# An expert layer behind linear attention: the last rows, the counting and the results in a new order of issue

## The chip, the cores and the metric

The kernel runs on one core of one Trainium2 chip. The time is the device time of the launch in microseconds (us). A change of about 0.2% (2.2 us) is the smallest that repeated runs of this kernel can tell from none.

## What is computed

Four sequences of 2,048 tokens with 256 channels go through a layer norm, a causal linear attention with 16 heads and a residual sum, and then through a second layer norm and a mixture of 8 experts, of which each token uses two.

```python
x = x + linear_attention(layernorm(x), Wq, bq, Wk, bk, Wv, bv, Wo, bo)   # elu(q)+1, elu(k)+1, causal
h = layernorm(x)
logits = h @ router_w.T                       # 8 experts
top, idx = top_k(logits, 2); p = softmax(top)
out = x + sum over the two chosen e of p_e * (gelu(h @ w1[e].T + b1[e]) @ w2[e].T + b2[e])
```

All of it is float32. The layer norms have no learned scale.

## The kernel before

**Blocks.** The 8,192 tokens are cut into 16 blocks of 512. A block goes through `stage_a` (layer norm, q, k, v, denominators), `stage_b` (scores, causal product, state) and `stage_c` (output projection `px` at L594, residual sum, choice of the two experts, second layer norm, counting). One pass `s` of the main loop (L968) traces stage a of block s, stage b of block s-1 and stage c of block s-2, piece by piece in turn; there are 18 passes, and the last one, s = 17, holds only stage c of block 15.

**Rows.** `stage_c` ends in a counting: two small products `pc` (L651, L654) of the choice `sel` with a triangular matrix and with ones give each token's place in its expert's list; VectorE turns them into `slots` (L675), and eight indirect DMAs on GpSimd's queue (L679) write the normed rows with token number and weights into `rows` in DRAM. These DMAs are collected in `writes`.

**Slot tiles.** The experts work on tiles of 256 rows of one expert. 68 of them are in the main program, three more stand behind a runtime condition at the end. A slot tile j is: `fetch_rows` (L797-L804: expert and row number into registers of SyncE, then the load of `xs`), `fetch_in` (L814, w1 of the expert, 512 KB), `fetch_out` (L822 and L826, w2 and b2), `turned` (four transposes `pt_xs` at L835 and the copy `xT` at L836), `hidden` (16 products `ph` at L863 and the gelu at L869), `output` (16 products `py` at L880, the sum with b2 at L885, the scaling at L889) and `store` (two indirect DMAs with addition, L894, that add the results into the output in DRAM). Every `store` waits until the two DMAs of the store before it have landed, and until the blocks' x1 that have been traced so far have landed (`after(i, added[-1] + stored)`). Every `fetch_rows` waits for all `writes` that have been traced before it. SyncE's queue runs in the order of tracing; the other engines' orders are made at build time by a scheduler that takes priorities from the order of tracing, and `follow` adds an order between two instructions without a wait.

**Order of tracing.** `slot_tiles` is a generator. For each j it does, up to the first yield, `hidden(j)`, `turned(j + 1)`, `fetch_rows(j + 3)`, `fetch_in(j + 2)`, and up to the second yield `output(j - 1)`, the store of tile j - 2, and `fetch_out(j + 1)`. `Work.step` runs it to the next yield. The main loop spreads the steps over the pieces of the passes: as many as the rows that are complete allow, `limit = 2 * (open_tiles - 3)`. Before pass 17 there are 49 open tiles and 84 steps have been run, so that the limit of 92 leaves 8; from these pass 17 takes off `2 * HOLD`, and the rest runs after the main loop, behind the tracing of the last block's rows:

```python
if s == NBLK + 1:
    left = max(0, left - 2 * HOLD)
```

**Buffers.** `xs`, `w1`, `w2` and `b2` have three buffers each, the result `y` four.

Of the kernel before, what the change touches and what calls it, by code (L numbers as in the profile page):

```python
# [13 lines left out]
ALU = mybir.AluOpType  # L14
# [10 lines left out]
def kernel(  # L25
# [132 lines left out]
    def ins_of(i):  # L158
        return getattr(i, "ins", i)

    def follow(inst, other):

        tc.add_manual_dep(
            ins_of(inst), ins_of(other).name,
            mybir.DependencyInfo(
                mybir.DependencyClass.NoSync, mybir.DependencyReason.SCHED_ONLY
            ), reason="order of issue",
        )

    QUIET = ROUND_ENDS[0] + 2  # L170

    def layernorm(src, dst, root_of=None, power=False, behind=None):

        st = small.tile([P, NT, 6], F32, tag="st", name="st")
        mv = small.tile([P, NT, 2], F32, tag="mv", name="mv")
        for t in range(NT):
            i = nc.vector.bn_stats(st[:, t, :], src[:, t, :])  # L179
            if behind:  # L180
                follow(i, behind[0])
            nc.vector.bn_aggr(mv[:, t, :], st[:, t, :])
        rstd = small.tile([P, NT], F32, tag="rstd", name="rstd")
        nc.vector.tensor_scalar_add(rstd, mv[:, :, 1], LN_EPS)
        if power:
            root = small.tile([P, NT], F32, tag="root", name="root")
            nc.gpsimd.tensor_tensor(root, rstd, neghalf, ALU.pow)
        else:

            half = small.tile([P, NT], I32, tag="half", name="half")  # L190
            nc.vector.tensor_single_scalar(
                half, rstd.bitcast(I32), 1, op=ALU.logical_shift_right
            )
            guess = small.tile([P, NT], I32, tag="guess", name="guess")
            nc.vector.tensor_scalar(guess, half, -1.0, float(0x5F3759DF), ALU.mult, ALU.add)
            root = guess.bitcast(F32)
            error = small.tile([P, NT], F32, tag="error", name="error")
            for _ in range(3):
                nc.vector.scalar_tensor_tensor(error, root, -0.5, root, ALU.mult, ALU.mult)
                nc.vector.tensor_tensor(error, error, rstd, ALU.mult)  # L200
                nc.vector.scalar_tensor_tensor(root, error, 1.5, root, ALU.add, ALU.mult)
        if root_of is not None:
            nc.vector.tensor_tensor(root_of, rstd, root, ALU.mult)
        rstd = root
        shift = small.tile([P, NT], F32, tag="shift", name="shift")
        i = nc.vector.scalar_tensor_tensor(
            shift, mv[:, :, 0], -1.0, rstd, ALU.mult, ALU.mult
        )
        if behind is not None:
            behind[:] = [i]  # L210
        for t in range(NT):
            if t % 2:
                nc.scalar.activation(  # L213
                    dst[:, t, :], src[:, t, :], AF.Identity,
                    bias=shift[:, t : t + 1], scale=rstd[:, t : t + 1],
                )
# [365 lines left out]
    def stage_c(n: int):  # L582
# [30 lines left out]
        for r in range(2):  # L613
            top = small.tile([P, NT], F32, tag=f"top{r}", name="top")
            nc.vector.tensor_reduce(top, lg, AX.X, ALU.max)
            eq = small.tile([P, NT, E], F32, tag=f"eq{r}", name="eq")
            nc.vector.tensor_tensor(eq, lg, wide(top), ALU.is_equal)
            nc.vector.tensor_tensor(eq, eq, prio_b, ALU.mult)
            first = small.tile([P, NT], F32, tag=f"first{r}", name="first")
            nc.vector.tensor_reduce(first, eq, AX.X, ALU.max)  # L620
            nc.vector.tensor_tensor(sel[:, :, r, :], eq, wide(first), ALU.is_equal)
            if r == 0:
                nc.vector.scalar_tensor_tensor(
                    lg, sel[:, :, 0, :], -3.0e38, lg, ALU.mult, ALU.add
                )
            tops.append(top)
        yield
        xn2 = att.tile([P, NT, R], F32, tag="xn2", bufs=3, name=f"xn2_{n}")
        rstd = layernorm(x1, xn2[:, :, 0:D])


        ed = small.tile([P, NT], F32, tag="ed", name="ed")
# [15 lines left out]
        sel_f = sel.rearrange("p t k e -> p (t k e)")  # L648
        M = 2 * NT
        pc = bank([P, 2, M, E], "pc")  # L650
        nc.tensor.matmul(  # L651
            pc[:, 0].rearrange("p m e -> p (m e)"), before, sel_f, start=True, stop=True
        )
        nc.tensor.matmul(  # L654
            pc[:, 1].rearrange("p m e -> p (m e)"), ones, sel_f, start=True, stop=True
        )
# [126 lines left out]


    plans = {}

    def slot_tiles(todo):

# [66 lines left out]
        def hidden(j):  # L855
            xT, w1t, bias = (state[j][key] for key in ("xs", "w1", "bias"))
            hT = moe.tile([P, NFC, ST], F32, tag="hT", name="hT")
            for f2 in range(NFC // 2):
                ph = bank([P, 2, ST], "ph")
                for i in range(2):  # L860
                    f = 2 * f2 + i
                    for cc in range(NCC):
                        nc.tensor.matmul(  # L863
                            ph[:, i, :], w1t[:, cc, ts(f, P)], xT[:, cc, :],
                            start=(cc == 0), stop=(cc == NCC - 1),
                        )
                for i in range(2):
                    f = 2 * f2 + i
                    nc.scalar.activation(  # L869
                        hT[:, f, :], ph[:, i, :], AF.Gelu, bias=bias[:, f : f + 1]  # L870
                    )
            state[j]["hT"] = hT

        def output(j):
            mine = state.pop(j)
            w2t, b2t, hT, to, wt = (mine[key] for key in ("w2", "b2", "hT", "to", "wt"))
            py = bank([P, NS, D], "py")
            for a in range(NS):
                for f in range(NFC):
                    nc.tensor.matmul(  # L880
                        py[:, a, :], hT[:, f, ts(a, P)], w2t[:, f, :],
                        start=(f == 0), stop=(f == NFC - 1),
                    )
            yt = moe.tile([P, NS, D], F32, tag="y", bufs=4, name=f"y_{j}")
            nc.vector.tensor_tensor(  # L885
                yt, py, b2t.unsqueeze(1).to_broadcast([P, NS, D]), ALU.add
            )
            for a in range(NS):
                nc.vector.tensor_scalar_mul(yt[:, a, :], yt[:, a, :], wt[:, a : a + 1])  # L889

            def store():
                mine = []
                for a in range(NS):
                    i = ins_of(nc.gpsimd.indirect_dma_start(  # L894
                        out=out_rows, in_=yt[:, a, :], in_offset=None, compute_op=ALU.add,
                        bounds_check=T - 1, oob_is_err=False,
                        out_offset=bass.IndirectOffsetOnAxis(ap=to[:, a : a + 1], axis=0),
                    ))

                    apart(i, f"out{len(added)}")  # L900
                    tc.add_to_no_dep_group("out", i)
                    after(i, added[-1] + stored)
                    mine.append(i)
                added.append(mine)

            return store
# [13 lines left out]
        for j in range(J + 1):  # L920
            if j < J:
                hidden(j)
            if j + 1 < J:
                turned(j + 1)
            if j + LEAD < J:
                fetch_rows(j + LEAD)
            if j + LEAD - 1 < J:
                fetch_in(j + LEAD - 1)
            if j < J:
                yield  # L930
            if j > 0:
                wait.append(output(j - 1))
            while len(wait) > (j < J):
                wait.pop(0)()
            if j + 1 < J:
                fetch_out(j + 1)
            if j < J:
                yield

    begins = {n - 1: r for r, n in enumerate(ROUND_ENDS)}
    HOLD = 5

    class Work:

# [21 lines left out]
    for s in range(NBLK + 2):  # L968
# [18 lines left out]
        while gens:  # L987
            for it in list(gens):
                if next(it, "end") == "end":
                    gens.remove(it)  # L990
                i += 1
                while ran < share and ran * order < i * share:
                    work.step()
                    ran += 1
# [58 lines left out]
```

## Time and profile before

| what | value |
|---|---|
| median of 4 runs | 1097.31 us (1096.05 to 1098.62) |
| the profiled execution's own time | 1101.44 us |
| its span, first to last instruction | 1099.7 us |
| TensorE busy, mean granted clock | 1022.6 us (93%), 0.957 |
| VectorE busy | 766.5 us (70%) |
| GpSimd busy (its indirect DMAs' issue) | 394.0 us (36%) |
| ScalarE busy | 385.3 us (35%) |
| store DMAs (L894) | 136, 1593 ns of GpSimd each, 4.4 us to landing |
| row DMAs (L679) | 128, 973 ns of GpSimd each, 2.6 us to landing |

The profile is one execution, and times inside it are counted from the start of its span. A line of the timeline has start, duration, engine, source line, operation, what is written from what, a count, and in brackets the idle time of the engine before it with what ended that idle time. A line of the table of waits has the waiting engine and line, what it waited for, the sum in us, how often, and the longest. In the table of windows each engine has its busy time and, in brackets, its instructions; behind them come the granted TensorE clock, the mean busy share of the 16 DMA engines and GB/s.

### The profile page before, as it was taken

The numbers are of one execution on the slowest core, as the hardware profiler recorded it, in microseconds if no ns is written. First come the engines' busy times: TensorE is split into PE (matmuls) and PEld (weight loads), VectorE is DVE, ScalarE is ACT, GpSimd is POOL, SyncE is SP. The second block draws the span as 40 slices with busy tenths as digits, with TensorE's granted clock in tenths as the row PEclk, the third lists the DMA queues.
The fourth block names the chain that finished last, engine by engine and source line by source line (L and its number), as shares of the span: only waits on it lengthen the run. The fifth ranks groups of instructions, "written<-read, shape, count | busy, mean of one in ns | idle before, by whom it ended". The sixth has DMA issues, their size and how long they took to land.

```text
span 1099.7 us, 23082 instructions
## 1 busy us (share of the span) xinstructions
PE 1022.6 (93%) x8358; PEld 816.0 (74%) x8358; DVE 766.5 (70%) x2600; ACT 385.3 (35%) x824; POOL 394.0 (36%) x308
## 2 busy tenths in 40 slices
PE   5897987989999999999999999999999889999993
PEld 3565665666767787878878887878788768888883
DVE  6769779879597959796888789796777633333331
ACT  3434333335252535243433435252532111222220
POOL 5003043132232444435351525243334543344434
PEclk9878988889899999999999999999999989999997
DMA  6001111534333556564646474645556589898873
GB/s 212 1 16 44 59 59 40 169 121 107 117 87 128 138 166 157 154 166 111 170 118 201 108 203 113 194 99 179 126 155 160 136 246 232 228 240 236 231 181 39
DMA packets 128722, 155.22 MB, mean 141 GB/s; under 512 B 9952, under 2 KB 105952, under 8 KB 128608
## 3 DMA queue, kind: packets, MB, share of 16 engines
q1 hardware_dynamic: 85680, 102.06, 29.7%
q0 software_dynamic: 25728, 34.88, 17.5%
q10 hardware_dynamic: 17200, 16.79, 4.8%
q8 instruction: 67, 1.10, 0.4%
q14 instruction: 47, 0.39, 0.1%
HBM read 108.05 MB, written 45.65 MB: 140 GB/s over the span
## 4 chain that ended last, share of the span: by engine, by line
PE 65%; DVE 22%; DMA 4%; issue 2%; POOL 1%; ACT 1%; SPq 0%; POOLq 0%; DVEq 0%
PE ph L863 19%; PE py L880 17%; DVE at L511 5%; PE pn L534 5%; PE pp L401 4%; PE sc L506 4%; DMA out_dram<-y,to 4%; PE pv L426 3%; PE px L594 3%; PE pn L527 3%; PE pt_xs L835 2%; DVE st L179 2%; DVE z L411 2%; PE pr L471 1%; DVE kT L343 1%
## 5 line engine op out<-in xcount | busy, mean ns | idle before, releaser
L894 POOL DMA_INDIRECT out_dram<-y,to x136 | 216.7, 1593 | 440.8 <-DVE y L885 121.0
L863 PE MATMUL ph<-xT,w 128*128 128x256 f32 x1088 | 256.2, 390 | 5.6 <-DMA w<-in_w_dram 5.2
L880 PE MATMUL py<-w,hT 128*128 128x256 f32 x1088 | 248.0, 381 | 0.0
L863 PEld LDWEIGHTS ph<-xT,w 128*128 128x128 f32 x1088 | 208.1, 195 | 41.9 <-issue 7.7
L880 PEld LDWEIGHTS py<-w,hT 128*128 128x128 f32 x1088 | 202.9, 190 | 28.7 <-issue 2.6
L869 ACT ACTIVATE hT<-ph,b1t 128x256 f32<-128x256 f32 x272 | 113.5, 469 | 223.2 <-PE ph L863 216.5
L511 DVE TENSOR_TENSOR at<-sc,causal 128x512 f32<-128x512 f32 x256 | 158.3, 679 | 11.1 <-PE sc L506 11.1
L679 POOL DMA_INDIRECT rows<-xn,slots x128 | 124.6, 973 | 94.0 <-DVE slots L675 51.4
L836 DVE COPY xT<-pt_xs 128x512 f32<-128x512 f32 x68 | 46.7, 687 | 143.3 <-PE pt_xs L835 143.3
L885 DVE TENSOR_TENSOR y<-py,b 128x512 f32<-128x512 f32 x68 | 47.0, 691 | 86.3 <-PE py L880 86.2
L506 PE MATMUL sc<-qM,kT 32*128 32x256 f32 x1024 | 79.2, 410 | 5.2 <-ACT share L436 5.2
L534 PE MATMUL pn<-at,vpad 128*32 128x128 f32 x2048 | 77.3, 297 | 0.0
L497 ACT ACTIVATE qM<-qs,parity 128x256 f32<-128x256 f32 x128 | 56.3, 498 | 58.3 <-DVE qs L476 46.1
L506 PEld LDWEIGHTS sc<-qM,kT 32*128 32x128 f32 x1024 | 49.4, 189 | 30.7 <-issue 8.2
L541 ACT COPY vT<-pn 128x256 f32<-128x256 f32 x64 | 23.7, 370 | 130.3 <-PE pn L534 130.3
L534 PEld LDWEIGHTS pn<-at,vpad 128*32 128x32 f32 x2048 | 57.6, 118 | 9.4 <-issue 2.0
L594 PE MATMUL px<-wo_sb,vT 128*128 128x264 f32 x256 | 64.1, 406 | 0.0
L426 PE MATMUL pv<-wv_sb,xnT 128*128 128x264 f32 x256 | 64.0, 406 | 0.0
L401 PE MATMUL pp<-xnT,wk_sb 128*128 128x512 f32 x128 | 60.3, 615 | 0.2 <-ACT xnT L336 0.2
L594 PEld LDWEIGHTS px<-wo_sb,vT 128*128 128x128 f32 x256 | 49.4, 198 | 12.7 <-issue 3.5
L232 POOL TENSOR_TENSOR x<-x,bo_bc 128x1024 f32<-128x1024 f32 x16 | 42.2, 2638 | 45.3 <-ACT xn L213 38.2
L401 PE MATMUL pp<-xnT,wq_sb 128*128 128x512 f32 x128 | 58.2, 597 | 0.0
(169 smaller groups left out, 1319.0 us busy)
## 6 DMA issues: line engine op xcount, KB each, us to landing
w<-in_w_dram SPq DMA_DIRECT2D x136, 512.0 KB, 4.6
xs<-rows SPq DMA_DIRECT2D x68, 260.0 KB, 3.0
b<-in_b_dram SPq DMA_DIRECT2D x68, 128.0 KB, 4.8
out_dram<-x ACTq DMA_DIRECT2D x16, 512.0 KB, 3.0
x<-in_x_dram ACTq DMA_DIRECT2D x15, 512.0 KB, 4.0
rows<-none SPq DMA_DIRECT2D x1, 2340.0 KB, 7.7
out_dram<-y,to POOLq DMA_INDIRECT x136, 4.4
rows<-xn,slots POOLq DMA_INDIRECT x128, 2.6
```

The source lines that it names most:

```text
L401: nc.tensor.matmul(pp, w[:, cc, ts(m, P)], xnT[:, cc, :], start=(cc == 0), stop=(cc == NCC - 1),)
L426: nc.tensor.matmul(pv, xnT[:, cc, ts(t, P)], wv_sb[:, cc, :], start=(cc == 0), stop=(cc == NCC - 1),)
L497: nc.scalar.activation(qM[:, :, par, :], qs[:, :, ts(c, P)], AF.Copy, scale=parity[:, par : par + 1],)
L506: nc.tensor.matmul(sc[g][:, m, :, :], kT[part, m, ts(c, P)], qM[part, m, :, :], start=True, stop=True,)
L511: nc.vector.tensor_tensor(at[:, g].rearrange("p m r i -> p (m r) i"), sc[g].rearrange("p m r i -> p (m r) i"), causal.unsqueeze(1).to_broa ...
L534: nc.tensor.matmul(pn[W * g : W * g + W, m, :], vp[:, c, NG * m + g, W * par : W * par + W], at[:, g, m, par, :], start=False, stop=(par = ...
L594: nc.tensor.matmul(px, vT[:, cc, ts(t, P)], wo_sb[:, cc, :], start=(cc == 0), stop=(cc == NCC - 1),)
L679: s = ins_of(nc.gpsimd.indirect_dma_start(out=rows[:, :], out_offset=bass.IndirectOffsetOnAxis(ap=slots[:, 2 * t + k : 2 * t + k + 1], axi ...
L863: nc.tensor.matmul(ph[:, i, :], w1t[:, cc, ts(f, P)], xT[:, cc, :], start=(cc == 0), stop=(cc == NCC - 1),)
L869: nc.scalar.activation(hT[:, f, :], ph[:, i, :], AF.Gelu, bias=bias[:, f : f + 1])
L880: nc.tensor.matmul(py[:, a, :], hT[:, f, ts(a, P)], w2t[:, f, :], start=(f == 0), stop=(f == NFC - 1),)
L894: i = ins_of(nc.gpsimd.indirect_dma_start(out=out_rows, in_=yt[:, a, :], in_offset=None, compute_op=ALU.add, bounds_check=T - 1, oob_is_er ...
```

## The change

Four edits. In the slot tiles, `fetch_rows(j + 3)` moves from the first half of step j to the end of the second, behind `fetch_in(j + 2)`, the store and `fetch_out(j + 1)`. In pass 17, `HOLD` is 7 in place of 5, and one step is run by hand after the second piece of stage c, which is the choice `sel`. For the last block, the second layer norm's reciprocal root is put behind the choice on VectorE, and the first counting product behind the last slot tile product that has been traced. Every store that is traced after the last block's rows is put behind the last of their DMAs on GpSimd's queue.

```diff
-    def layernorm(src, dst, root_of=None, power=False, behind=None):
+    def layernorm(src, dst, root_of=None, power=False, behind=None, last=None):
...
-        nc.vector.tensor_scalar_add(rstd, mv[:, :, 1], LN_EPS)
+        i = nc.vector.tensor_scalar_add(rstd, mv[:, :, 1], LN_EPS)
+        if last is not None:
+            follow(i, last)
...
-            nc.vector.tensor_tensor(sel[:, :, r, :], eq, wide(first), ALU.is_equal)
+            selected = nc.vector.tensor_tensor(
+                sel[:, :, r, :], eq, wide(first), ALU.is_equal
+            )
...
-        rstd = layernorm(x1, xn2[:, :, 0:D])
+        rstd = layernorm(
+            x1, xn2[:, :, 0:D], last=selected if n == len(blocks) - 1 else None
+        )
...
-        nc.tensor.matmul(
+        i = nc.tensor.matmul(
             pc[:, 0].rearrange("p m e -> p (m e)"), before, sel_f, start=True, stop=True
         )
+        if n == len(blocks) - 1:
+            follow(i, multiplied[0])
...
+    multiplied = [None]
...
-                        nc.tensor.matmul(
+                        multiplied[0] = nc.tensor.matmul(
                             ph[:, i, :], w1t[:, cc, ts(f, P)], xT[:, cc, :],
...
-                    nc.tensor.matmul(
+                    multiplied[0] = nc.tensor.matmul(
                         py[:, a, :], hT[:, f, ts(a, P)], w2t[:, f, :],
...
             def store():
                 mine = []
+                finished = len(writes) == 2 * NT * len(blocks)
...
+                    if finished:
+                        tc.add_manual_dep(i, writes[-1].name, BEHIND, reason="order of issue")
...
-            if j + LEAD < J:
-                fetch_rows(j + LEAD)
             if j + LEAD - 1 < J:
                 fetch_in(j + LEAD - 1)
...
             if j + 1 < J:
                 fetch_out(j + 1)
+
+            if j + LEAD < J:
+                fetch_rows(j + LEAD)
...
-    HOLD = 5
+    HOLD = 7
...
+                if s == NBLK + 1 and i == 2:
+                    work.step()
```

More of the change, by code (lines that the diff above doesn't have):

```diff
@@ L159, in ins_of @@
         return getattr(i, "ins", i)
+    BEHIND = mybir.DependencyInfo(
+        mybir.DependencyClass.NoSync, mybir.DependencyReason.SCHED_ONLY
+    )
     def follow(inst, other):
         tc.add_manual_dep(
[L164 to L167, printed above, removed]
+            ins_of(inst), ins_of(other).name, BEHIND, reason="order of issue"
         )
     QUIET = ROUND_ENDS[0] + 2
-    def layernorm(src, dst, root_of=None, power=False, behind=None):
+    def layernorm(src, dst, root_of=None, power=False, behind=None, last=None):
         st = small.tile([P, NT, 6], F32, tag="st", name="st")
@@ L628, in stage_c @@
         xn2 = att.tile([P, NT, R], F32, tag="xn2", bufs=3, name=f"xn2_{n}")
-        rstd = layernorm(x1, xn2[:, :, 0:D])
+        rstd = layernorm(
+            x1, xn2[:, :, 0:D], last=selected if n == len(blocks) - 1 else None
+        )
         ed = small.tile([P, NT], F32, tag="ed", name="ed")
```

## The prediction

> **What bounds the kernel now.** I read the windows first, then TensorE's waits, then GpSimd's timeline, and the chain of waits last. From 350 to 850 us TensorE is busy 499.62 of 500 us at a granted clock of 1.00: nothing but less TensorE work could shorten that stretch. The last block breaks it. TensorE's waits from 700 us on, and two windows:
>
> ```profile
> PE ph L863 <- DMA w<-in_w_dram: 5.2, 1, 5.2
> PE pc L651 <- DVE error L199: 3.5, 1, 3.5
> ...
> 880.00:890.00 10.00, 7.99 (x39) 6.68 (x38) 7.56 (x26) 1.68 (x4) 7.62 (x7) 1.00 0.41 107
> 890.00:900.00 10.00, 6.77 (x22) 5.61 (x23) 0.12 (x1) 1.40 (x4) 3.11 (x2) 0.66 1.01 316
> ```
>
> The counting `pc` waits 3.5 us at 870.94 for the choice, and `ph` of tile 43 waits 5.2 us at 893.23 for its w1. The weights come late because SyncE's queue stood: `fetch_rows(44)`, traced behind the last block's eight row DMAs, waited for their landing, and w1(43) and w2(42) were queued behind it. The timeline has both engines:
>
> ```profile
> 872.03 1.57 POOL L894 DMA_INDIRECT out_dram<-y,to  x1 [8.54 <-DVE guess L201]
> 873.91 1.55 POOL L894 DMA_INDIRECT out_dram<-y,to  x1 [0.30 <-DVE ends L676]
> 875.77 0.99 POOL L679 DMA_INDIRECT rows<-xn,slots  x1 [0.30 <-issue]
> ...
> 884.70 0.96 POOL L679 DMA_INDIRECT rows<-xn,slots  x1 [0.30 <-issue]
> 885.96 1.61 POOL L894 DMA_INDIRECT out_dram<-y,to  x1 [0.30 <-DVE b1t L777]
> 887.88 1.57 POOL L894 DMA_INDIRECT out_dram<-y,to  x1 [0.30 <-issue]
> 896.11 1.56 POOL L894 DMA_INDIRECT out_dram<-y,to  x1 [6.66 <-DMA out_dram<-y,to]
> ```
>
> ```profile
> 887.50 0.38 SPq L802 DMA_DIRECT2D xs<-rows  x1
> ...
> 888.09 0.37 SPq L814 DMA_DIRECT2D w<-in_w_dram  x1
> ```
>
> Counting back from the last pair, the pair at 872.03 is the store of tile 39 (its `y` was ready at 861.4, the store waited for the last block's x1 to land), that at 885.96 is tile 40. So one store pair stands ahead of the last rows, and the others behind. What decides the end is on the same queue. GpSimd's waits from 886 us, the last three pairs, and the end of the chain:
>
> ```profile
> POOL out_dram L894 <- DMA out_dram<-y,to: 98.1, 24, 6.7
> ```
>
> ```profile
> 1078.11 1.55 POOL L894 DMA_INDIRECT out_dram<-y,to  x1 [3.05 <-DMA out_dram<-y,to]
> 1079.97 1.55 POOL L894 DMA_INDIRECT out_dram<-y,to  x1 [0.30 <-DVE y L885]
> 1084.56 1.55 POOL L894 DMA_INDIRECT out_dram<-y,to  x1 [3.04 <-DVEq L1004]
> 1086.41 1.55 POOL L894 DMA_INDIRECT out_dram<-y,to  x1 [0.30 <-issue]
> 1090.92 1.55 POOL L894 DMA_INDIRECT out_dram<-y,to  x1 [2.95 <-DMA out_dram<-y,to]
> ```
>
> ```profile
> 1071.55 21.72 DMA out_dram<-y,to
> ```
>
> 24 of the 27 pairs after 886 start when the pair before has landed; tiles' results lie ready 4 to 6.8 us earlier from tile 46 on (66: ready 1080.6, stored 1084.56). From 885.96 to 1090.92 this chain makes 27 steps, 204.96 us, 7.59 each. TensorE, one tile in 7.345 us (`y` at 940.06, 947.41, 954.75), ends at 1082.6. The two chains run side by side, and the stores are the later one.
>
> **The change part by part.** *HOLD.* Pass 17 has 92 - 84 = 8 steps left; 8 - 10 and 8 - 14 are both below nothing, so 7 in place of 5 does nothing. What keeps tiles apart is the one hand-run step: `hidden(41)`, `turned(42)`, `fetch_in(43)` are now traced before the last rows.
>
> *Counting behind the product.* `ph` of tile 41 starts after `px`, at 867.3 instead of 871.82, and covers the choice (ready 870.8). Its 16 products end about 870.8, `pc` follows at once. Gone from TensorE: 3.5 us of wait, and 1.2 us because this `ph` ran 4.93 after the wait where 3.72 is usual. The order on VectorE puts the root's 12 dependent steps (0.21 each by the plan's chain, 875.34 to 876.41 in five) behind the choice: root at 873.5 instead of 871.25, the scaled rows at about 875.3. The slots were ready at 874.95. So the first row DMA stands where it stood, 875.77, minus 0.5 because no store holds the queue until 875.46, plus up to 1 if the copy `xT` (0.69) and the root meet on VectorE. I take 0; eight times 1.27 us end at 885.7 and `fetch_rows(44)` goes out at 887.5 as before.
>
> *Rows behind weights.* When SyncE now stands at `fetch_rows(44)`, w1(43) and w2(42) have been issued, one tile more than before. They go out from 862 to 866 us, into a stretch whose DMA share is 0.40 from 870 on. TensorE therefore runs `ph` 43 and `py` 42 through to about 890.5 and waits for w1(44), issued at 888.1 and landed like the one in the profile after 5.0 us: `ph` 44 starts where `ph` 43 started, 893.2. TensorE is one tile, 7.35 us, ahead for the rest; the wait left is 893.2 - 890.5 = 2.7 us, an estimate. If `pt_xs` 44 is queued ahead of `py` 42, the same wait falls earlier and costs at most 1.2 us more. Through the other blocks the move makes 13 row loads wait for eight more row DMAs (tiles 3, 5, 7, 10, 14, 18, ... 42). Each would go out with the next one of before, for example tile 38 at 810.49 instead of 778.69, landed 3.0 us later, needed by `pt_xs` at 822.32. The shortest distance I find is 5.8 us (tile 42, out at 862.0, landed 865.0, needed at 870.8). What stands behind them on SyncE is the same w1 and w2 as before. Cost 0; without this cover a block would cost what its row load comes too late.
>
> The granted clock after the waits: 0.83 in 870 to 880 and 0.66 in 890 to 900, and `ph` at 893.23 took 6.17 us instead of 3.62. After the shorter wait I charge between 0 and that 2.55, but nothing of it reaches the sum, since TensorE isn't last. [...]
>
> *Results behind the last rows.* This is the dear part. The pair of tile 39 moves from 872.03, where the queue was free for it, to behind the rows, where tile 40 started: 885.96. From there the chain has 28 steps instead of 27. Queued behind it are all later stores, and behind these the end. The loads that slow the landings keep their times from 887.5 on, with tile numbers one higher, and stop one tile earlier. So I let the pairs start at the old times up to 1034.85 (then tile 58, before 59). The steps of before from there are 7.20, 7.60, 8.13, 7.09, 6.68, 6.56, 6.45, 6.36, shrinking as the loads stop. With the loads ending a tile earlier the 7.20 drops out and three steps of 6.36 stand at the end instead of one: 48.87 + 2 x 6.36 = 61.59, and the last pair starts at 1034.85 + 61.59 = 1096.4 instead of 1090.92: **+5.5 us**. The results then lie about 20 us before their store (1096.4 against 1084.0 - 7.35 = 1076.7). With four `y` buffers, a `y` is written 28 us after the one four tiles earlier was ready, so with about 7 us for a pair to land this just fits; the spare 2.1 us of VectorE before `xT` hides the rest.
>
> Bounds of the step's length: all 28 at the mean 7.59 give 1098.5 (+7.6); a rows start 1 us late makes +8.6. Below, 6.4 a step, the unloaded end, would put the chain at 1065, and TensorE's one tile would decide: its results at 1076.7, last pair near 1079.6, -11.3.
>
> The nearest rows for how loads slow a landing: 2.95 to 3.05 us of wait at a DMA share of 0.33, 3.1 to 4.6 at about 0.9, 6.66 at 1.01. The move of the row loads splits one burst (974.54, 975.11, 976.78, 977.51 in the profile) into w1 at the end of `ph` and the rest 4 us later, the same bytes per tile. I keep the old step, with bounds of 0.3 us either way, 28 x 0.3 = 8.4. [...]
>
> **The sum.** Profiled execution: 1101.44 + 5.5 = 1106.9. The median of the runs is 4.13 us below the profiled execution; I carry the difference over unchanged: 1097.31 + 5.5 = 1102.8.
>
> **The rivals.** *A, faster: the stores' chain gets shorter steps.* The place is 886 to 940 us, where six steps took 10.15, 9.45, 7.78, 7.74, 9.06 and 10.03, 54.2 in all, against 7.28 on average in the 13 after. One tile's weights already lie there, and the new burst may let pairs land before it. It decides when the first 19 steps lose over 5.5 us, that is 0.29 each. At 7.28 for the first six the chain gains 10.5 and the end comes 5 us before the old one: 1092.3, and TensorE's tile allows 1090.0. For it: the slow steps lie under a share over 0.9. Against it: from 887.5 on three tiles' loads are still issued together. 22%.
>
> *B, no difference:* about half of that saving, or a lag given back at the end, within 2.2 us: 1097.3. 15%.
>
> *C, the change doesn't do what it says:* true for HOLD, priced at 0. For the stores it would need the scheduler to ignore the order; then tile 39 stays at 872 and the chain is the old one: within B.
>
> *D, the `y` buffers:* if pairs start over 21 us late, `output` waits, TensorE with it, and loads space out; the chain stays the bound, so at most the +8.6 above.
>
> **How the numbers follow.** The forecast and D hold 63%, own range 1099.6 to 1106.5. The whole range goes from TensorE's one tile, 1090.0, to 28 steps at 7.59 with late rows and a rounding, 1106.5. About 0.2% (2.2 us) can be told from none by repeated runs: faster 0.22, same 0.15, slower 0.63.
>
> **What would show it.** Right: TensorE's 3.5 us wait at `pc` gone, one wait of some 3 us at `ph` 44 near 893; the eight row DMAs on GpSimd unbroken from about 875.8 and only then tile 39; pairs waiting for landings to the end; last `py` near 1075, last pair near 1096. Wrong: a store before the last rows, rows starting before 874, loaded steps under 7.3 from 886 to 940, or a last pair within a step of its `y`.

## The result and the profile after

The changed kernel takes 1.0027 of the time before (95% interval 1.0009 to 1.0044), that is 2.9 us more on 1096.8 us (1.0 to 4.8). The medians are 1102.59 us of 44 runs against 1096.81 us of 70; 18 of the 44 lie at 1106 to 1132 us, where one of the 70 does; the ratio leaves them out, no profile shows them, and why the changed kernel has them stays open. The direction and the place were as forecast, the size was about half of the 5.5 us.

The profiled execution took 1097.32 us, span 1095.6. It stands below the profiled one of before (1101.44) because the stretch ahead of the last block was shorter: `px` of the last block starts at 857.37 us here and at 863.61 there. In the ten profiles up to e8 it starts anywhere from 852.7 to 863.6; e8, which differs from the changed kernel in the number of `y` buffers alone, has 863.2. So everything below is counted from this `px`. From `px` to the end before takes 236.1 us, after 238.2: **+2.1 us**.

TensorE's waits from 700 us on, and the windows that correspond to those of before (shifted by the 6.24 us between the two `px`):

```profile
PE pt_xs L846 <- DMA xs<-rows: 5.6, 1, 5.6
PE pn L530 <- DVE S L559: 0.8, 1, 0.8
PE ph L874 <- DVE y L896: 0.4, 1, 0.4
```

```profile
873.76:883.76 10.00, 6.03 (x28) 4.96 (x27) 6.50 (x25) 1.68 (x4) 8.01 (x7) 0.94 0.37 100
883.76:893.76 10.00, 8.40 (x32) 7.29 (x33) 2.36 (x7) 0.52 (x2) 3.12 (x2) 0.72 0.97 293
```

The 3.5 us at `pc` and the 5.2 us at `ph` are gone; one wait of 5.6 us is left, and it stands at `pt_xs`: the transposes of tile 44 were queued ahead of `py` 42. TensorE's timeline there, with the two loads on SyncE that it waits for:

```profile
876.17 3.62 PE L874 MATMUL ph<-xT,w 128*128 128x256 f32 x16
885.36 1.09 PE L846 MATMUL pt_xs<-ident,xs 128*128 128x128 f32 x4 [5.57 <-DMA xs<-rows]
886.24 5.18 PE L891 MATMUL py<-w,hT 128*128 128x256 f32 x16
891.25 3.62 PE L874 MATMUL ph<-xT,w 128*128 128x256 f32 x16
```

```profile
881.88 0.38 SPq L813 DMA_DIRECT2D xs<-rows  x1
882.51 0.37 SPq L825 DMA_DIRECT2D w<-in_w_dram  x1
```

`py` 42 takes 5.18 us where 3.62 is usual, at a granted clock of 0.72 in this window. All the same TensorE is ahead: the last `y` is ready 214.7 us after `px` instead of 220.4.

GpSimd's queue does what was forecast. Eight row DMAs in one run, no store ahead of them, tile 39 behind:

```profile
870.00 0.99 POOL L689 DMA_INDIRECT rows<-xn,slots  x1 [11.90 <-DVE xn L644]
...
878.91 0.98 POOL L689 DMA_INDIRECT rows<-xn,slots  x1 [0.30 <-issue]
880.19 1.62 POOL L906 DMA_INDIRECT out_dram<-y,to  x1 [0.30 <-issue]
882.11 1.57 POOL L906 DMA_INDIRECT out_dram<-y,to  x1 [0.30 <-issue]
890.20 1.57 POOL L906 DMA_INDIRECT out_dram<-y,to  x1 [6.52 <-DMA out_dram<-y,to]
```

The rows start 12.6 us after `px` (before: 12.2). From 880.19 the pairs make 28 steps, and they wait for landings to the end: GpSimd's waits, the last three pairs, and the end of the chain:

```profile
POOL out_dram L906 <- DMA out_dram<-y,to: 99.0, 25, 6.5
```

```profile
1074.25 1.55 POOL L906 DMA_INDIRECT out_dram<-y,to  x1 [3.01 <-DMA out_dram<-y,to]
...
1080.61 1.55 POOL L906 DMA_INDIRECT out_dram<-y,to  x1 [2.95 <-DMA out_dram<-y,to]
...
1086.96 1.55 POOL L906 DMA_INDIRECT out_dram<-y,to  x1 [2.94 <-DMA out_dram<-y,to]
```

```profile
1067.83 21.48 DMA out_dram<-y,to
```

28 steps take 206.8 us (7.38 each), where before had 27 in 205.0 (7.59).

**A quantity that the prediction read and did not use** decides the rest: the lag of a pair, from the end of its `y` on VectorE to its start on GpSimd. Tile 52 (counted back from the last pair), VectorE's line and GpSimd's:

```profile
965.64 0.62 DVE L900 TENSOR_SCALAR y<-y,wt 128x256 f32<-128x256 f32 x2
```

```profile
982.54 1.55 POOL L906 DMA_INDIRECT out_dram<-y,to  x1 [4.18 <-DMA out_dram<-y,to]
```

The `y` ends at 966.26, the pair starts at 982.54: a lag of 16.3 us. It is nearly the same for every tile as long as loads run. The profiles of this study with both stores of a tile, one per row; the last `y` and the last pair are in us after `px`:

| kernel | lag at tile 46 | 50 | 54 | 58 | last `y` ready | lag of tile 67 | last pair |
|---|---|---|---|---|---|---|---|
| before | 6.1 | 6.2 | 5.2 | 5.7 | 220.4 | 6.9 | 227.3 |
| before, second (e14) | 0 | 0 | 0 | 0 | 221.6 | 3.0 | 224.6 |
| before, third (e19) | 0 | 0 | 0.3 | 0 | 220.7 | 3.0 | 223.7 |
| e6 | 6.4 | 6.7 | 6.1 | 5.7 | 221.2 | 7.2 | 228.4 |
| e17 | 5.5 | 6.1 | 5.2 | 5.2 | 221.9 | 6.3 | 228.2 |
| e2 | 13.0 | 12.8 | 13.0 | 12.7 | 220.3 | 13.5 | 233.8 |
| e1 | 8.4 | 8.7 | 9.0 | 8.8 | 219.3 | 9.1 | 228.4 |
| e3 | 8.7 | 8.5 | 8.8 | 9.4 | 222.6 | 13.2 | 235.8 |
| after | 16.0 | 16.3 | 16.4 | 16.5 | 214.7 | 14.9 | 229.6 |
| after, second (e13) | 16.1 | 16.2 | 17.1 | 16.3 | 216.7 | 15.3 | 231.9 |
| after, third (e18) | 16.2 | 15.8 | 16.8 | 16.4 | 214.7 | 16.0 | 230.7 |
| e7 | 9.1 | 12.2 | 15.6 | 17.2 | 215.5 | 15.6 | 231.1 |
| e15 | 8.7 | 11.3 | 15.1 | 16.3 | 214.8 | 14.5 | 229.2 |
| e8 | 16.0 | 15.9 | 17.1 | 17.6 | 216.4 | 19.4 | 235.8 |
| e12 | 9.7 | 9.0 | 7.0 | 5.0 | 215.5 | 3.0 | 218.4 |
| e21 | 12.8 | 13.5 | 12.4 | 12.6 | 215.4 | 13.9 | 229.3 |
| e20 | 6.6 | 6.2 | 6.0 | 5.5 | 214.5 | 7.1 | 221.6 |

Last pair is last `y` plus lag. Before to after that is -5.7 + 8.0 = +2.3 us. Averaged over tiles 46 to 58 the lag is 5.9 us before and 16.3 after; lags without a tile number below are such averages. (The profiles of e3 and e8 are of their longest executions, so their last pairs, at 235.8, are no typical ones.)

### The profile page after: what moved, and what is told of

The parts are those of the page before. It is cut to its first block, busy times and chain, and to the rows that moved or that the text cites. A ratio compares the mean times of both kernels' runs of the same rounds, so it can differ in the third digit from the quotient of the medians.

```text
span 1095.6 us, 23073 instructions
## 1 busy us (share of the span) xinstructions
PE 1012.1 (92%) x8358; PEld 808.8 (74%) x8358; DVE 767.4 (70%) x2600; ACT 385.1 (35%) x824; POOL 393.5 (36%) x308
## 3 DMA queue, kind: packets, MB, share of 16 engines
q0 software_dynamic: 25728, 34.88, 17.6%
## 4 chain that ended last, share of the span: by engine, by line
PE 58%; DVE 25%; DMA 4%; issue 3%; POOL 2%; ACT 2%; DVEq 0%; POOLq 0%; SPq 0%; ACTq 0%
PE ph L874 18%; PE py L891 16%; DVE at L514 6%; PE pn L537 4%; DMA out_dram<-y,to 3%; PE pv L429 3%; PE sc L509 3%; PE pp L404 3%; DVE z L414 2%; PE pn L530 2%; PE pt_xs L846 2%; DVE st L180 2%; PE px L597 2%; DVE kT L346 2%; DVE x L601 1%
## 5 line engine op out<-in xcount | busy, mean ns | idle before, releaser
L874 PE MATMUL ph<-xT,w 128*128 128x256 f32 x1088 | 252.4, 386 | 3.0 <-DVE y L896 2.9
L874 PEld LDWEIGHTS ph<-xT,w 128*128 128x128 f32 x1088 | 205.6, 192 | 38.5 <-DVE y L896 5.9
L880 ACT ACTIVATE hT<-ph,b1t 128x256 f32<-128x256 f32 x272 | 113.5, 469 | 226.9 <-PE ph L874 220.3
L597 PE MATMUL px<-wo_sb,vT 128*128 128x264 f32 x256 | 61.1, 392 | 0.0
L429 PEld LDWEIGHTS pv<-wv_sb,xnT 128*128 128x128 f32 x256 | 49.7, 199 | 9.6 <-issue 0.5
```

The lines of the kernel that those rows point to most:

```text
L429: nc.tensor.matmul(pv, xnT[:, cc, ts(t, P)], wv_sb[:, cc, :], start=(cc == 0), stop=(cc == NCC - 1),)
L597: nc.tensor.matmul(px, vT[:, cc, ts(t, P)], wo_sb[:, cc, :], start=(cc == 0), stop=(cc == NCC - 1),)
L874: multiplied[0] = nc.tensor.matmul(ph[:, i, :], w1t[:, cc, ts(f, P)], xT[:, cc, :], start=(cc == 0), stop=(cc == NCC - 1),)
L880: nc.scalar.activation(hT[:, f, :], ph[:, i, :], AF.Gelu, bias=bias[:, f : f + 1])
```

## The experiments

Theory 1 was the prediction's: the chain of pairs sets the end, and one pair more behind the rows costs a step. Theory 2: TensorE sets the end, and the loss comes from the moved row loads. Later, when both were settled, the question was what sets the lag. In e12 to e21 the kernel before took about 1205 us instead of 1097 (in the profiles of these runs the granted clock was 0.92 to 0.93 over the span instead of 0.95 to 0.97, and `px` came at 965 to 979 us instead of 853 to 864). One chip gave both, 1097.4 us with e5 to e8 and 1204.4 with e20 and e21, so the chip alone doesn't make the difference. Each ratio is against runs of before taken with it.

### Which part of the change costs what

**e1_results_free**: the changed kernel without the order "results behind last rows".

```diff
-                finished = len(writes) == 2 * NT * len(blocks)
...
-                    if finished:
-                        tc.add_manual_dep(i, writes[-1].name, BEHIND, reason="order of issue")
```

> The change without its last edit: stores may again stand ahead of the last rows on GpSimd, as the scheduler likes, and the store of tile 39 does. Theory 1 (the stores' chain behind the last rows sets the end; one pair more in it is one step of 6.4 to 7.6 us): 27 steps instead of 28, so 6 us less than the change, a ratio of about 0.9975 to the kernel before, with the last pair some 206 us after the last row DMA less one step. Theory 2 (TensorE sets the end and the stores only trail; the loss comes from the moved row loads): no difference to the change, 1.003.

Measured: ratio 0.9983 (0.9951 to 1.0015), 27 steps of 7.43. Tile 39 stands ahead of the rows again, but goes out 13.8 us after `px` instead of 8.4, and the rows start at 17.5 instead of 12.2. It waits for the last block's x1 to land, and that store now has two tiles of weights ahead of it. The x1 stores of the changed kernel, from issue to landing; the longest is the last block's:

```profile
DMA to landing us min/median/max: 2.9/3.0/8.5
```

(In e2, with one tile of loads ahead of it, the last of them issued 4.3 us earlier, the same store took 3.3 us.) So two parts of the change collide, and the order of the results hides it.

**e2_results_only**: the kernel before with that order alone.

```diff
+                finished = len(writes) == 2 * NT * len(blocks)
...
+                    if finished:
+                        tc.add_manual_dep(i, writes[-1].name, BEHIND, reason="order of issue")
```

> The kernel before with the last edit alone: every store traced after the last rows stands behind them on GpSimd. Theory 1: one step more, with the kernel before's long first steps: 5.5 to 7.5 us more, 1.005 to 1.007. Theory 2: 1.000, since TensorE's order and its waits are untouched.

Measured: ratio 1.0042 (1.0014 to 1.0069), +4.6 us (1.5 to 7.6); theory 2's 1.000 is outside. The last `y` stays at 220.3, the lag is 13.2 us instead of 5.9: one tile of TensorE (7.35) more, from a single pair.

**e3_weights_only**: the kernel before with the row load behind the weights alone.

```diff
-            if j + LEAD < J:
-                fetch_rows(j + LEAD)
             if j + LEAD - 1 < J:
                 fetch_in(j + LEAD - 1)
...
             if j + 1 < J:
                 fetch_out(j + 1)
+            if j + LEAD < J:
+                fetch_rows(j + LEAD)
```

> The kernel before with only the row loads moved behind the weights. TensorE should keep its 3.5 us wait at the counting and lose the 5.2 us wait for w1 of tile 43. Theory 1: the chain still has 27 steps behind the last rows, and only its first seven may shorten, by the 2.7 us by which they did in the change: 0.9975 to 1.000. Theory 2: TensorE is one tile ahead, 7.35 us less: 0.9935; or, if the moved loads are what costs, 1.003.

Measured: ratio 1.000 (0.9968 to 1.0032). The collision of e1 is here too (tile 39 at 14.1, rows from 17.8). The 3.5 us at `pc` stay, as expected, but the 5.2 us at `ph` 43 make way for 5.7 us at `pt_xs`: TensorE gets no lead from this edit alone, its last `y` is at 222.6. The profile is of the longest execution (1104.33 against a median of 1098.51); the lag of 8.4 to 9.4 from tile 46 to 58 agrees with e1's 8.4 to 9.7.

### Is it the pairs?

**e4_half_after** and **e5_half_before**: one of the two store DMAs of each tile left out.

```diff
-                for a in range(NS):
+                for a in range(1):
```

> The change with one of the two store DMAs of every tile left out, so half of the experts' results are not added: the chain's step shrinks to about 1.9 us of issue and 3 to 4.6 us of landing, below TensorE's 7.35. Theory 1: the end then follows TensorE, whose last result lies ready 15 us before its store in the change: some 16 us less than the change, 0.987 of the kernel before. Theory 2: only the last DMA's issue and a little landing are saved, 3 to 5 us: 0.998 to 1.000.

> The kernel before with the store of a tile's second half left out (its output is therefore not the reference's), the partner of e4_half_after. With half of the stores the chain of pairs cannot be the bound in either kernel, so this pair shows what the change does to TensorE alone. Theory 1 (the stores' chain set the end in both full kernels; on TensorE the change is a gain): the last product ends 216 to 217 us after the last block's px, as in the kernel before, against 213.4 in e4_half_after; from px to the end 227 to 229 us, 3 to 4 us later than e4_half_after (224.3). Ratio to the kernel before about 0.984, if e4's 0.981 is taken and 3.3 us are added. Theory 2 (the moved loads hurt TensorE or the loads, and that is where the change loses): px to the end 224 us or less, ratio 0.981 or less.

Measured: 0.9809 (0.9769 to 0.9849) and 0.9916 (0.9886 to 0.9946). From tile 50 (e4) and 42 (e5) on nearly every store starts when its `y` is ready. A tile of e4, on VectorE and on GpSimd:

```profile
975.71 0.62 DVE L900 TENSOR_SCALAR y<-y,wt 128x256 f32<-128x256 f32 x2
```

```profile
976.34 1.57 POOL L906 DMA_INDIRECT out_dram<-y,to  x1 [5.78 <-DVE y L900]
```

`px` to the end is 224.3 and 228.2 us, so with the pairs off the path the change is a **gain** of 3.9 us on TensorE, where the full kernels show a loss. That is theory 1. (The two ratios differ by some 12 us; they are from different chips, and in the two profiles 4.1 us more lie ahead of `px`.)

**e8_ybufs_after**: six buffers for `y`.

```diff
-            yt = moe.tile([P, NS, D], F32, tag="y", bufs=4, name=f"y_{j}")
+            yt = moe.tile([P, NS, D], F32, tag="y", bufs=6, name=f"y_{j}")
```

> The changed kernel with six buffers for y instead of four. Theory 1 (the chain of pairs sets the end by its own landings): last pair 229 to 230 us after px, ratio to the kernel before 1.002 to 1.004, as the changed kernel. Rival D of the prediction (the pairs lie so late that the four buffers hold back VectorE and TensorE, and with them the chain): the last product ends earlier than 213.4 us after px and the last pair 1 to 3 us earlier, ratio 1.000 to 1.001; or TensorE's earlier loads make the steps longer, ratio above 1.004.

Measured: 1.0048 (1.0015 to 1.0080); the last `y` is not earlier (216.4 against 214.7). Rival D falls: two more buffers give nothing back.

### Can the pair be saved?

**e6_seen_before**: the kernel before, with row loads waiting only for the row DMAs known when their round was planned.

```diff
-                plans[r] = plan(r)
-            where, te, b1t, behind = plans[r]
+                plans[r] = plan(r), len(writes)
+            (where, te, b1t, behind), seen = plans[r]
...
-            after(i, writes + cleared)
+            after(i, writes[:seen] + cleared)
```

> The kernel before, but a row load waits only for those row DMAs that had been traced when its round was planned. SyncE therefore does not stand at the row load of tile 44 while the last block's rows are written; the loads behind it are not bunched up, and the order on GpSimd is that of before (tile 39 ahead of the rows, 27 pairs behind). Theory 1 (chain of pairs; its first six steps of 54.2 us are long because a burst of loads held back by the stalled queue lies beside them): those six steps fall to 45 to 48 us, the chain to 196 to 199 us, ratio 0.992 to 0.995. If the long first steps have another cause (the low clock, the rows' own traffic), the chain stays at 203 to 206 us and the ratio at 0.999 to 1.001, and only TensorE's 5.2 us wait at tile 43 is gone. Theory 2: TensorE gains 5 us and the end with it, whatever the chain does, ratio 0.995.

Measured: 0.9996 (0.9964 to 1.0028). The lever missed: tile 44 is the first of the last round, whose plan counts the last rows, so its row load still goes out 25.5 us after `px`. It says nothing of the slow first steps (54.0 us for six, 54.2 in the kernel before).

**e7_store39_early**: the changed kernel with the store of tile 39 ahead of the last block, where it waits for no x1.

```diff
-            while len(wait) > (j < J):
+            while len(wait) > (j < J and j != 40):
```

> The changed kernel with the store of tile 39 traced one tile earlier, ahead of the last block, so that it neither waits for the last block's x1 nor stands behind the last rows. Theory 1 (one pair more behind the rows costs one step of 7.4 us): 27 pairs behind the rows, the rows start where they do in the changed kernel, 12.6 us after px, last pair 222 to 223 us after px instead of 229.6; ratio to the kernel before 0.996 to 0.998 (the 7.4 us less of 2.9 us of loss and up to 1 us). Theory 2: the end stays 238 us after px, ratio 1.002 to 1.003.

Measured: 0.9989 (0.9956 to 1.0022). The rows start at 12.6 and one pair fewer stands behind them, as meant, but the last pair comes at 231.1. Between tiles 48 and 56 the lag slides from 8.9 to 16.2: the saved tile is given back. Pairs 48 to 50 there:

```profile
946.30 1.55 POOL L906 DMA_INDIRECT out_dram<-y,to  x1 [3.97 <-DMA out_dram<-y,to]
...
955.61 1.55 POOL L906 DMA_INDIRECT out_dram<-y,to  x1 [5.90 <-DVE wt L855]
...
964.33 1.55 POOL L906 DMA_INDIRECT out_dram<-y,to  x1 [5.31 <-DMA out_dram<-y,to]
```

Steps of 9.3 and 8.7 us. (The releaser `wt` on the middle line is of another tile; this pair's `y` had been ready for over 8 us, so it was the landing.)

### Do the loads set the step?

**e12_tail_kept**: no weights or biases loaded from tile 47 on.

```diff
+            if j >= 47:
+                state[j]["w1"] = kept["w1"]
+                return
...
+            if j >= 47:
+                state[j]["w2"], state[j]["b2"] = kept["w2"], kept["b2"]
+                return
```

> The changed kernel with no weights and output biases loaded from tile 47 on; those tiles use the ones of tile 46, so the output is not the reference's. TensorE's work is the same. Theory 1, loads setting the step: from about 75 us after px the DMA share falls from 0.9 to 0.4 or less, the steps fall from 7.4 to 6.3 to 6.5 us until the pairs have caught up with TensorE (some 14 us of lag at 1 us a step), then 7.35; the end comes from TensorE, 224 to 226 us after px, ratio 0.987 to 0.990. If the pairs' landing times are their own affair and not the loads': steps and end as in the changed kernel, ratio 1.003.

Measured: 1.0010 (0.9980 to 1.0039), where the unaltered changed kernel taken with it (e13) has 1.0088. A window of 110 us from 80 us after `px`, the changed kernel and then this one; the last two columns are DMA share and GB/s:

```profile
937.37:1047.37 110.00, 110.00 (x541) 96.91 (x540) 38.84 (x120) 25.10 (x60) 46.61 (x30) 1.00 0.93 234
```

```profile
1056.38:1166.38 110.00, 110.00 (x541) 96.89 (x540) 39.23 (x120) 25.16 (x60) 49.85 (x32) 1.00 0.47 73
```

With the share at 0.47 most steps are 6.4 to 7 us, the lag melts from 9.7 to 0, and from tile 64 on the pairs wait for `y`. `px` to the end is 227.2 us against e13's 240.7, the direction of theory 1 at less than its size (224 to 226, ratio 0.987 to 0.990). The loads hold the pairs up: with them, at a share of 0.93, the lag stays at 16.3 us.

**e15_b2_resident** and **e17_b2_before**: the eight experts' output biases held on chip from tile 43 on, 9% fewer bytes per tile, on e7 and on the kernel before. (e11, the same with a buffer of its own for the biases, needed 10.4 KB of on-chip memory per partition where 7.6 were left, and has no result.)

```diff
+            if j >= BEFORE_ALL:
+                at = nc.vector.value_load(b2t, min_val=0, max_val=E - 1)
+                b2t = b2_all[0][:, ds(at * D, D)]
```

> The kernel of e7 (the changed kernel with the store of tile 39 ahead of the last block) with all eight output biases loaded once, just ahead of the row load of tile 44, into a buffer of the attention that is free by then; from tile 43 on no bias is loaded, VectorE reads the expert's number into a register and adds the bias from there. Each tile then loads 128 KB less, of 1412. Theory 1, with the DMA engines' load as what sets the step of the chain of pairs: where the pairs lie behind TensorE the loaded step falls by 0.3 to 0.6 us below 7.35, so they catch up by some 6 to 10 us before the loads stop; px to the end 226 to 232 us against 238 to 240, ratio to the kernel before 0.989 to 0.995. If the step does not depend on how much is loaded: as e7, 0.997 to 0.999. If VectorE's register read is dear (over 2 us a tile), it shows as a wait of TensorE, and the ratio is above 1.

> The kernel before with the same resident biases from tile 43 on, its order otherwise untouched. Theory 1: the pairs, one fewer behind the rows than in the changed kernel, catch up with TensorE well before the end, which then comes from TensorE: last product 217 to 220 us after px, last pair 4 to 5 us later, px to the end 229 to 232 us, ratio 0.993 to 0.996, so 1 to 4 us behind e15, whose TensorE is ahead. If the step does not depend on the loads: 1.000.

Measured: 1.0042 (1.0013 to 1.0071) and 1.0011 (0.9983 to 1.0039). Both expectations fall. The middle steps are those of the parents (7.95 in e15 as in e7's 7.96, 7.37 in e17), e15 slides from 8.7 at tile 46 to 16.1 at tile 56 as e7 did. So 9% fewer bytes don't show in the step; nothing between this and e12 was tried.

### What fixes the lag

**e13_after_again, e18_after_third, e14_before_again, e19_before_third**: both kernels unaltered.

> The changed kernel once more, unaltered, for a second profile of it and for a ratio on the same chip as e11. If the first profile's 206.8 us for 28 steps is what the kernel does, the second gives 204 to 209 us, the first seven pairs behind the rows 57 to 59 us, and px to the end 236 to 240 us. If the steps vary by chance from one execution to the next, the sum differs by more than 3 us, and the prediction's size was missed by a draw and not by a term. Ratio 1.001 to 1.005.

> The kernel before once more, unaltered, for a second profile of its chain. Steps fixed by the kernel: 27 steps in 203 to 207 us, first six in 53 to 55.5 us, tile 39 at 8.4 us after px. By chance: a sum outside of that.

> The changed kernel a third time, for its ratio to the kernel before on one chip and a third profile. If the kernel fixes its steps: 28 steps in 206 to 208 us, last pair 229 to 232 us after px. Ratio 1.001 to 1.005 on a chip where the kernel before takes 1097 us, 1.005 to 1.012 on one where it takes 1205.

> The kernel before a third time, for a third profile of its chain. If its steps vary by execution: 27 steps anywhere from 200 to 206 us, the middle twelve 7.35 each. If the first profile was the rule and the second the exception: 204 to 206 us.

Measured: ratios 1.0088 (1.0049 to 1.0127) for e13 and 1.0124 (1.0079 to 1.0169) for e18. The changed kernel repeats itself: 28 steps in 206.8, 207.5 and 207.6 us, lag 16.3 or 16.4. The kernel before does not: 27 steps in 205.0, 201.6 and 201.5. In the second and third profile its pairs have caught up with TensorE after three or four steps, and stay within 1 us of it up to tile 66. The second's `y` on VectorE, its pair, and GpSimd's waits there from 990 us on:

```profile
1040.61 0.62 DVE L889 TENSOR_SCALAR y<-y,wt 128x256 f32<-128x256 f32 x2
```

```profile
1041.24 1.55 POOL L894 DMA_INDIRECT out_dram<-y,to  x1 [3.93 <-DVE y L889]
```

```profile
POOL out_dram L894 <- DVE y L889: 100.5, 25, 6.6
POOL out_dram L894 <- DMA out_dram<-y,to: 8.8, 2, 5.7
```

Here the pair goes out 0.01 us after its `y`, and the queue that waited 24 times for landings in the first profile waits 25 times for VectorE. TensorE sets the end of these two, and the change then moves the last pair by 7.1 us (231.9 and 230.7, mean 231.3, against 224.6 and 223.7, mean 224.2). What the two ratios have beyond these 7 us (3 to 8 us) is in none of the profiles and stays open.

**e20_once_early** and **e21_weights_once**: the row load behind the weights for tile 44 alone, in e20 with e7's early store.

```diff
+            if j + LEAD < J and j != 41:
+                fetch_rows(j + LEAD)
             if j + LEAD - 1 < J:
                 fetch_in(j + LEAD - 1)
...
-            if j + LEAD < J:
+            if j == 41:
                 fetch_rows(j + LEAD)
```

> The changed kernel with the row load behind the weights for tile 44 alone (all other row loads stand ahead of the weights again, as before), and with the store of tile 39 ahead of the last block as in e7. If the fixed lag comes from the order of the loads: TensorE is as far ahead as in the changed kernel (last result ready 214 to 216 us after px), the lag settles at 5.9 us or less, last pair 217 to 222 us after px, px to the end 226 to 231 us, ratio to the kernel before 0.992 to 0.997 on a chip where that takes 1097 us, 0.995 to 1.000 on one where it takes 1205. If the lag has nothing to do with the order: it settles at 8.8 or slides to 16.2 as in e7, px to the end 233 to 240 us.

> The changed kernel with the row load behind the weights for tile 44 alone. If the lag comes from the order of the loads: it settles at 13.0 us, as in e2, with TensorE as in the changed kernel; last pair 227 to 229 us after px, 3 us earlier than in the changed kernel, ratio about 1.000 on a chip where the kernel before takes 1097 us, 1.003 to 1.007 on one where it takes 1205. If not: lag 16.2, ratio as the changed kernel's on that chip.

Measured: 0.9979 (0.9953 to 1.0005) and 1.0052 (1.0025 to 1.0079). The lags came as expected, 6.0 us (5.3 to 6.9) and 13.0 us (12.4 to 14.4), in place of the new order's 9 and 16.3, with TensorE as far ahead as in the changed kernel. Tile 50 of e20, on VectorE and on GpSimd:

```profile
1064.73 0.62 DVE L900 TENSOR_SCALAR y<-y,wt 128x256 f32<-128x256 f32 x2
```

```profile
1071.53 1.55 POOL L906 DMA_INDIRECT out_dram<-y,to  x1 [4.49 <-DMA out_dram<-y,to]
```

A lag of 6.2 us. Nor did e20 slide as e7 did. `px` to the end is 230.3 us: shorter than in all three profiles of before (236.1, 233.2, 232.4) and of after (238.2, 240.7, 239.4). That is 8 to 10 us less than the changed kernel's profiles; against the kernel before it is 2.5 us (0.0021 of 1204.4), with an interval that just takes in 1.

## Why the prediction was right in direction and wrong in size

**Right.** In the profile that the prediction read, the end hangs on the pairs and not on TensorE (e4, e5); `HOLD` did nothing, since the steps left are below zero either way; the wait at `pc` is gone; the rows start within 0.5 us of where they stood; tile 39 moved behind them and made 28 steps of 27. That this order alone costs one step holds: e2 shows +4.6 us (1.5 to 7.6), and a lag larger by 7.35 us.

**Wrong: the old times for the chain's starts, and with them the size of its steps, 210.5 us for 28 in the sum, 206.8 measured.** The step that failed is "So I let the pairs start at the old times up to 1034.85". The first 19 steps took 146.6 us and not 148.9, the last nine 60.2 and not 61.6, and the rows stood 0.5 us later: 5.5 - 2.3 - 1.4 + 0.5 is the 2.3 us by which the last pair moved. With it fell "nothing of it reaches the sum, since TensorE isn't last": at the same lag and the same pairs behind the rows, a TensorE 4.9 us ahead (last `y` at 215.4 in e21, 220.3 in e2) has its last pair 4.5 us earlier, and one 5.9 us ahead (214.5 in e20, 220.4 before) has it 5.7 us earlier.

The prediction took a landing's length to belong to its place in time. The profiles show something else. While loads run, the twelve steps after the first seven average 7.32 to 7.40 us in 12 of the 16 profiles that keep their stores and their weight loads, TensorE's 7.345 a tile (e3 and e8 7.48; e7 and e15, which slide, 7.95): the pairs keep a fixed lag behind TensorE. Counted by lag, with the averages over tiles 46 to 58, the change comes out as follows:

- one pair more: +7.35 (e1 to after, e20 to e21, before to e2: 7.3, 7.1 and 7.35 measured);
- the new order of the loads: +3.1 (before to e3 and e1: 5.9 to 8.9 and 9.0; e2 and e21 to after: 13.2 and 13.0 to 16.3). The prediction weighed this edit at 0 for the step, and the step did stay; the lag at which it stays did not. The trace of before holds one order of loads only, so no row of it gives this term;
- a longer end without loads: -2.5. From its average to tile 67 the lag goes from 16.3 to 14.9 after and from 5.9 to 6.9 before; after, the last six steps are 6.4 each, where the prediction took 6.68, 6.56, 6.45 and three of 6.36;
- TensorE ahead: -5.65, and not the 7.35 of one tile that the prediction expected (and left out of the sum). The wait left was 5.6 us and not 2.7, with `pt_xs` 44 ahead of `py` 42 (the case that the prediction priced at 1.2 more) and a slow `py` behind it, so `ph` 44 starts 33.9 us after `px` and not where `ph` 43 stood, at 29.6; but it takes 3.62 us where that took 6.17. 7.35 - 4.3 + 2.55 is 5.6.

7.35 + 3.1 - 2.5 - 5.65 is 2.3, the 2.3 us between the last pairs. This adds up what was measured; it was not a forecast. In the prediction's own numbers the pairs were to end 19.7 us behind the last `y` (1096.4 against 1076.7); they ended 14.9 behind.

**The rivals.** A's shorter steps came, with less weight: the first 19 lost 2.3 us, less than the 5.5 at which it decides. B's "lag given back at the end" is the -2.5 above, and its bound of 2.2 us lies inside the interval of the result (1.0 to 4.8). D is refuted by e8. C held for `HOLD` alone. What no rival had: that before itself runs at two lags, 0 and 5.9. From the one profile shown the chain of before looked like the kernel's own; two of three profiles have TensorE as the bound, and there the same change moves the last pair by 7.1 us instead of 2.3. Both of these were taken where before takes 1205 us, the one with 5.9 where it takes 1097; e17, with a lag of 5.4 beside them, speaks against that as the cause, and nothing here settles it. So that the size came out near half of the forecast is in part luck: it depends on which lag before has.

**The wait, and the order of the loads.** The wait of 5.57 us in front of `pt_xs` was followed by transposes of 1.09 us instead of 0.60 and a `py` of 5.18 instead of 3.62, at a clock of 0.72 in the window. No wait of 2.7 us came, so no run shows the 0 to 2.55 us that the prediction charged behind one, an estimate. The changed kernel loads the same bytes as e21 in another order on SyncE, and the lag differs by 3 us (13.0 in e21, 16.3 after). That the step stays when the bytes per tile stay was the author's estimate; measured, the mean of the twelve steps does (7.33 in e21, 7.39 after) and the lag does not.

## What to carry to other kernels

When a chain of dependent DMAs runs beside a loop that loads once per tile, don't price it as steps times length: read for several tiles how far it lies behind its producer, in more than one execution, and price a change by whole tiles of lag (here one pair more was 7.1 to 7.35 us, a tile 7.345). An early start of such a chain is worth nothing if the lag slides back (from 8.9 to 16.2 us in e7), and the loads' place in the loop alone moved the lag by about 3 us (13.0 in e21, 16.3 after). Test two edits that touch the same queues apart: here the moved row loads alone delayed the store that stood ahead of the rows and gave TensorE no lead (e3), and with that store out of the rows' way TensorE is 4.9 (e7) to 5.7 us (after) ahead.

## What was not expected of the hardware

- The lag of the pairs takes few values: 0, 5.4 to 6.1 and 13.0 to 13.2 us where a tile's loads leave in the order row load, w1, w2, b2 (before, e2, e6, e14, e19, e20, e21, and e17 without b2), 8.9 to 9.0 and 16.3 to 16.5 where it is w2, b2, row load, w1 (e1, e3, e8 and the three profiles of after). In either order the two values above 0 lie about one tile of TensorE (7.35 us) apart. The prediction had the burst split in two; it was turned round, with the four still within 3.5 us. SyncE before and after:

```profile
1040.66 0.37 SPq L802 DMA_DIRECT2D xs<-rows  x1
1041.22 0.37 SPq L814 DMA_DIRECT2D w<-in_w_dram  x1
1042.89 0.37 SPq L822 DMA_DIRECT2D w<-in_w_dram  x1
1043.62 0.34 SPq L826 DMA_DIRECT2D b<-in_b_dram  x1
```

```profile
1038.36 0.37 SPq L833 DMA_DIRECT2D w<-in_w_dram  x1
1039.09 0.35 SPq L837 DMA_DIRECT2D b<-in_b_dram  x1
1040.79 0.37 SPq L813 DMA_DIRECT2D xs<-rows  x1
1041.82 0.37 SPq L825 DMA_DIRECT2D w<-in_w_dram  x1
```

- A pair's place beside the loads is the same at both values of an order. From tile 46 to 58 a pair goes out on average 2.0 to 2.4 us behind the nearest row load in before, e2, e6, e20 and e21, and 0.5 to 0.6 us behind it in e1, e3 and the three profiles of after. In before the six of the 13 pairs that go out over 2.1 us behind the row load are followed by a step of 6.8 us on average, the seven others by one of 7.7; in after the six over 0.45 us behind it by 7.2, the others by 7.4. What makes the lag settle was not shown. Why e7 and e15 left 8.8 after tile 48, e1 stayed there, and what puts before at 0 or at 5.9 was not settled.
- 9% fewer bytes per tile changed no step (e15, e17); without weights and biases most steps were 6.4 to 7 us instead of 7.4 (e12).
- A store of 512 KB behind two tiles of loads took 8.5 us to land (6.7 to 9.9 in e1, e3, e4, e7 and e8) where 3.0 is the median.
